# A selective-scan stack on one core: delta's matmul moved one slot later, one stream piece moved from slot 0 to slot 3, statistics of the finished sums one slot later

## The chip, the cores and the metric

The kernel runs on one core of a Trainium2 chip. The metric is device time in microseconds (us), the median of several executions. The core has five engines that matter here: PE (TensorE, matmuls), DVE (VectorE), ACT (ScalarE), POOL (GpSimd) and SP (SyncE, which here only issues DMAs).

## What is computed

The input x is (16, 192, 64, 64) in float32. Four layers follow each other, each `x = x + layer(group_norm(x))`:

- layer 0: a small per-channel network with tanh (a likelihood), evaluated at x - 0.5 and x + 0.5;
- layer 1: a 5-point shift and a 960 to 192 channel matmul;
- layer 2: four selective scans over the 4096 pixels, row-wise and column-wise, each in both directions (K = 4 directions, N = 16 states per channel);
- layer 3: depthwise convolutions, a channel mix, batch norm over all images, and a clip.

The scans are what the change touches. Cut to the core:

```python
delta = softplus(dts + dt_projs_bias)
def step(h, inp):
    d, u, Bt, Ct = inp
    dA = exp(d[..., None] * A)
    h = dA * h + (d * u)[..., None] * Bt[:, :, None, :]
    y = einsum('bkdn,bkn->bkd', h, Ct)
    return (h, y)
```

The outputs of the four directions are added, with the column-wise ones transposed back.

## The kernel before, in words

Two images form a pair: 2 x 192 channels are NT = 3 tiles of 128 partitions. For each of the 8 pairs `scans` runs layer 2 and, in the same loop, the *front* (statistics, layers 0 and 1, projection and split) of the next pair; then `layer3` runs. The first front runs alone before the loop, and the last pair has no front beside its scans. A last pass over all pairs does the batch norm and the clip.

**Slots and blocks.** `scans` walks over `todo`: tile j, direction k in the order 1, 3, 0, 2, and 4 chunks of LC = 1024 pixels. That is 48 *blocks* t of 16 *slots* n, one slot per state, so 768 slots s a pair. Within `scans` every engine keeps program order (`_InOrder`), so the loop from line 998 is an order written out by hand for each queue. One slot does, in this order:

- SP: `load_c(s + 2)`, the row of C broadcast to 128 partitions (tile cb, 4 buffers); in some slots also `load_bp`, `load_dt`, `load_xc`;
- DVE: `product(s)`, delta*u times B, in place in PSUM (tile pbt, 2 buffers), then whatever was handed to `E.later` (`E.between()` drains it), then the scan (`scan(s)`, tile h, 8 buffers);
- ACT: a copy of the scan's last column to `state`, then `decay(s + 3)`, the exponential dA (3 buffers);
- POOL: h times cb in place, and in every fourth slot a DMA that adds h of the slot before to it;
- PE: `spread(s + 2)`, two matmuls that spread B's row over the partitions into pbt;
- PE and ACT: `add_up(s - LATE)` with LATE = 4: the matmuls with the identity add h to `ysum` in PSUM; for the block's last state an ACT copy takes ysum to X or Xt. `ysum` has one buffer[...]. This call is made in slot 3 for the last state of the block before, and in slot 5 for the first sum of the block itself.

**Delta.** `step_rest(t + 1)` (lines 867 to 888) prepares the next block's delta: two matmuls into `v`, which takes the same PSUM buffer as `ysum` (tag "ysum"), an ACT softplus with bias to `delta` (with its own activation table, loaded before it, and the table of exp and tanh loaded again after it), and, at the next call in slot 8, `du` = delta*u on POOL. It is called in slot 3, right after `add_up` (lines 1023 to 1030). `load_dt(t + 2)` stands in slot 4 at the head of the loop; the tile `dt` has one buffer, which v reads.

**The stream.** `fr` is the next pair's front, a generator that yields pieces (lines 1032 to 1041). In layer 0 a piece is a quarter of a unit of 128 rows x 512 pixels: PE matmuls of two f32 products, the ACT tanhs or copies after them, and in places row loads by SP, a norm on ACT or a sigmoid. Slot 0 takes two layer-0 pieces, slots 3 and 5 none, all others one, and in slots 0 and 12 the statistics that a piece leaves behind are issued at once. In the other stages slots 0, 4, 8 and 12 take two units, 3 and 5 none, others one (a layer-1 matmul is half a unit, a projection step 0.36).

**Finishing.** When all four directions of a tile j are summed, `finish(j - 1)` (lines 963 to 980) adds Xt, transposed, to X in four parts: on POOL for the first two tiles, on DVE for the last. One step of it is made per slot from slot 5 on. Two steps after each add it hands the part's bn_stats (DVE) to `E.later`; after the last one it stores X by SP.

Of the kernel before, what the change touches and what calls it, by code (L numbers as in the profile page):

```python
# [104 lines left out]
def conv_preact_kernel(ctx: ExitStack, tc: tile.TileContext, a: dict):  # L105
# [5 lines left out]
    def row_tiles(ap):  # L111
        return ap.rearrange("(j p) l -> p j l", p=P)
# [199 lines left out]
    def image(ap):  # L312
        return ap.rearrange("p (h w) -> p h w", w=HW)

    def columns(ap):
        return ap.rearrange("p (h w) -> p w h", w=HW)
# [465 lines left out]
    def scans(i, o, st3, nxt):  # L782

        E = _Engines(tc, True)
        with ExitStack() as es:
# [14 lines left out]
            X = one.tile([P, L], F32, name="X")  # L800
# [12 lines left out]
            def seq(t, k, at, n):  # L813


                v = image(t) if k % 2 == 0 else columns(t)
                return v[:, at // HW : (at + n) // HW, :]

            def load_bp(t):
                if t < T:  # L820
                    j, k, at, first = todo[t]
                    bps[t] = two.tile([BP, LC], BF16, name="bp")
                    E.sp.dma_start(out=bps[t], in_=o.bp[k, :, at : at + LC])

            def load_dt(t):
                if t < T:
                    j, k, at, first = todo[t]
                    dts[t] = one.tile([32 + RD, 512], F32, name="dt")
                    src, r = (o.dtp, RD * (k // 2)) if k % 2 else (o.dt, RD * (2 + k // 2))
                    for h in range(2):  # L830
                        E.sp.dma_start(
                            out=dts[t][32 * h : 32 * h + RD, :],
                            in_=src[r : r + RD, at + 512 * h : at + 512 * h + 512],
                        )
# [6 lines left out]
            def norm_xn(j):  # L841
                if j < NT:
                    normalise(E.dve, xns[j], xns[j], o.gm, o.rstd, j)

            def load_xc(t):
                if t < T and todo[t][1] == 0:
                    j, k, at, first = todo[t]
                    xcs[t] = one.tile([P, LC], F32, name="xc")
                    E.sp.dma_start(out=xcs[t], in_=row_tiles(o.x2)[:, j, at : at + LC])

            def load_c(s):
                t, n = divmod(s, N)
                j, k, at, first = todo[t]
                cb = cbs[s] = cp.tile([P, LC], F32, name="cb")
                src, row = (o.c, 64 + 16 * k) if k % 2 == 0 else (o.cp, 16 * (k - 1))
                for b, rows in {
                    0: ((0, slice(0, P)),),
                    1: ((0, slice(0, 64)), (1, slice(64, P))),
                    2: ((1, slice(0, P)),),
                }[j]:  # L860
                    r = row + N * b + n
                    E.sp.dma_start(
                        out=cb[rows, :],
                        in_=src[r : r + 1, at : at + LC].to_broadcast([rows.stop - rows.start, LC]),
                    )

            def step_rest(t):


                j, k, at, first = todo[t]  # L870
                dt = dts.pop(t)
                v = py.tile([P, LC], F32, name="v", tag="ysum")
                for h in range(2):
                    rows = slice(32 * h, 32 * h + RD)
                    E.pe.matmul(
                        v[:, 512 * h : 512 * h + 512],
                        dtw[rows, k, j, :],
                        dt[rows, :],
                        start=True,
                        stop=True,  # L880
                    )
                delta = two.tile([P, LC], F32, name="delta")
                E.table(SOFTPLUS)
                E.act.activation(delta, v, AF.Softplus, bias=dtb[:, k, j : j + 1])
                yield
                du = two.tile([P, LC], F32, name="du")
                E.gps.tensor_tensor(image(du), image(delta), seq(xns[j], k, at, LC), ALU.mult)
                made[t] = delta, du

            def decay(s):  # L890
                t, n = divmod(s, N)
                j, k, at, first = todo[t]
                dA = dAs[s] = da.tile([P, LC], F32, name="dA")
                E.table(TANH)
                E.act.activation(dA, made[t][0], AF.Exp, scale=a_neg[:, k, j, n : n + 1])
# [14 lines left out]
            def product(s):  # L910
                E.dve.tensor_tensor(pbs[s], made[s // N][1], pbs[s], ALU.mult)

            def scan(s):
                t, n = divmod(s, N)
                j, k, at, first = todo[t]
                if (j, k) not in state:
                    state[j, k] = sp_.tile([P, N], F32, name="state")
                dA, pbt, cb = dAs.pop(s), pbs.pop(s), cbs.pop(s)
                back = k >= 2
                flip = slice(None, None, -1) if back else slice(None)  # L920
                h = hs[s] = hp.tile([P, LC], F32, name="h")
                v = state[j, k][:, n : n + 1]
                E.dve.tensor_tensor_scan(
                    h[:, flip], dA[:, flip], pbt[:, flip], 0.0 if first else v, ALU.mult, ALU.add
                )
                E.act.copy(v, h[:, 0:1] if back else h[:, LC - 1 : LC])
                E.gps.tensor_tensor(h, h, cb, ALU.mult)
                if n % 4 == 1:
                    E.gps.dma_start(out=h, in_=hs[s - 1], accum_op=ALU.add)
# [32 lines left out]

            def finish(j):

                for c in range(4):
                    x = X[:, 1024 * c : 1024 * c + 1024]
                    eng = E.gps if j < NT - 1 else E.dve
                    eng.tensor_tensor(
                        image(x), image(x), columns(Xt)[:, 16 * c : 16 * c + 16, :], ALU.add
                    )  # L970
                    yield
                    yield

                    def stats(c=c):
                        for h in range(2 * c, 2 * c + 2):
                            E.dve.bn_stats(st3[:, j, h, :], X[:, 512 * h : 512 * h + 512])

                    E.later(stats)
                yield
                E.sp.dma_start(out=row_tiles(x3_d[i])[:, j, :], in_=X)  # L980

            load_xn(0)
# [12 lines left out]
            kind = None  # L995
            fin = iter(())
            gstep = iter(())
            for s in range(total):
                t, n = divmod(s, N)
                j, k, at, first = todo[t]  # L1000
                if s + 2 < total:
                    load_c(s + 2)
                if n == 2:
                    load_bp(t + 1)
                if n == 4:
                    load_dt(t + 2)
                if n == 6:
                    load_xc(t + 1)
                product(s)
                E.between()  # L1010
                scan(s)
                if s + 3 < total:
                    decay(s + 3)
                if s + 2 < total:
                    spread(s + 2)
                if (t + 2) % (K * NC_) == 0 and n == 14:
                    load_xn(j + 1)
                if (t + 1) % (K * NC_) == 0 and n == 5:
                    norm_xn(j + 1)
                if n > 4:  # L1020
                    next(fin, None)

                if n == 3:
                    add_up(s - LATE)
                    if s >= LATE and (s - LATE + 1) % (K * NC_ * N) == 0:
                        fin = finish(j - 1)
                    gstep = step_rest(t + 1) if t + 1 < T else iter(())
                    next(gstep, None)
                elif n == 8:
                    next(gstep, None)  # L1030

                if kind == "l0":
                    for _ in range({0: 2, 3: 0, 5: 0}.get(n, 1)):
                        kind = next(fr, None) if kind == "l0" else kind
                        if n in (0, 12):
                            E.between()
                elif n not in (3, 5):
                    done = 0
                    while done < (1.99 if n % 4 == 0 else 0.99) and kind != "l0":
                        kind = next(fr, 1)  # L1040
                        done += kind if isinstance(kind, float) else 1
                if n != 3:
                    add_up(s - LATE)
# [293 lines left out]
```

## Time and profile before

| what | value |
| --- | --- |
| median of 3 executions | 28266.48 us (28245.82 to 28275.6) |
| profiled execution | 28295.17 us, span 28293.1 us |
| mean granted TensorE clock | 0.904 |
| DVE busy | 24223.9 us (86%) |
| PE busy | 23483.5 us (83%) |
| POOL busy | 20787.2 us (73%) |
| ACT busy | 16092.7 us (57%) |
| scans (DVE) | 6144 x, 2346 ns (with state) or 2285 ns (first chunk) |
| products (DVE) | 6144 x 1211 ns |
| adds of X and Xt on POOL | 64 x 3133 ns |
| softplus (ACT) | 384 x 1113 ns |
| activation table loads | 1104 x 1283 ns |

Pairs 0 to 6 take about 2998 us each from the first scan to the last, pair 7, without a front beside it, 2790 us. Seen from a pair's first scan, layer 0 of the next pair runs from some 107 to 1680 us, layer 1 from 1783 to 2290 us, the projection to 2475 us and the split to 2590 us.

How to read the lines: a line of the timeline gives start and duration in us, engine, line of the kernel (L64 is the helper that keeps program order, so one goes by the tiles' names), output<-inputs, shape, and in brackets the engine's idle time before it with what ended it. A line of the waits gives engine and tile, what it waited for, the total in us, the number of times, and the longest.

### The profile page before, as it was taken

To read this page: it belongs to the slowest core of one execution; us is meant where nothing else is said; L and a number is where in the kernel's file an instruction comes from. 1 tells how busy PE (TensorE), PEld (TensorE's weight loads), DVE (VectorE), ACT (ScalarE), POOL (GpSimd) and SP (SyncE) were. 2 spreads that over 40 slices of the span, in tenths; PEclk is the share of its full clock that TensorE was granted. 3 is DMA by queue.
4 is the path that set the end of the run, shared out by engine and by line. 5 is a ranking of instruction groups with operands and counts; after the bars stand their busy time and mean duration, and the time that the engine had idled before them with its cause. 6 is when DMAs were issued, how large, how long until landed. Compare 5 with 4: busy or idle time off the path is not lost. (4 is left out here: it accounts for less than half of the span.)

```text
span 28293.1 us, 208020 instructions
## 1 busy us (share of the span) xinstructions
PE 23483.5 (83%) x57140; PEld 9639.0 (34%) x57140; DVE 24223.9 (86%) x15397; ACT 16092.7 (57%) x23037; POOL 20787.2 (73%) x10440
## 2 busy tenths in 40 slices
PE   8799977999689986999779997799968998766663
PEld 4343323333233332333324332333323333222221
DVE  0399988998889988999989998899988998899994
ACT  7377445774467643775547744577446764344433
POOL 2388876887768876788768887688777887677772
PEclk9899988999899998999889998899989999888886
DMA  4479864897568973888748986489756897367765
GB/s 101 133 219 220 213 199 139 220 218 211 159 180 222 218 215 116 219 218 220 210 125 218 219 215 198 136 220 219 213 162 176 220 219 212 115 189 191 191 182 232
DMA packets 2008001, 5447.99 MB, mean 193 GB/s; under 512 B 550393, under 2 KB 550617, under 8 KB 1989425
## 3 DMA queue, kind: packets, MB, share of 16 engines
q1 hardware_dynamic: 1782192, 4578.95, 56.1%
q0 software_dynamic: 221184, 805.40, 14.9%
q10 hardware_dynamic: 3456, 50.33, 0.4%
q8 instruction: 455, 7.45, 0.1%
q14 instruction: 714, 5.84, 0.1%
HBM read 3896.19 MB, written 329.51 MB: 149 GB/s over the span
## 5 line engine op out<-in xcount | busy, mean ns | idle before, releaser
L64 POOL TENSOR_TENSOR h<-h,cb 128x1024 f32<-128x1024 f32 x6144 | 14853.6, 2465 | 4470.5 <-ACT state L64 3854.4
L64 DVE TENSOR_TENSOR_SCAN h<-dA,state,pbt 128x1024 f32<-128x1024 f32 x4608 | 10811.0, 2346 | 659.1 <-ACT dA L64 97.5
L64 PE MATMUL ysum<-h,ident 128*128 128x512 f32 x18432 | 9459.7, 638 | 191.6 <-DMA h<-h 144.7
L64 DVE TENSOR_TENSOR pbt<-du,pbt 128x1024 f32<-128x1024 f32 x6144 | 7441.2, 1211 | 852.4 <-PE pbt L64 812.1
L64 ACT ACTIVATE dA<-delta,t_alog 128x1024 f32<-128x1024 f32 x6144 | 7034.8, 1146 | 6.6
L64 PEld LDWEIGHTS ysum<-h,ident 128*128 128x128 f32 x18432 | 3780.8, 206 | 4474.2 <-issue 3926.6
L64 ACT COPY state<-h 128x1 f32<-128x1 f32 x6144 | 1141.0, 186 | 6533.9 <-DVE h L64 6508.4
L64 PE MATMUL pbt<-bp,pick 96*128 96x512 bf16 x8192 | 2729.3, 418 | 1942.8 <-DVE h L64 1931.8
L64 DVE TENSOR_TENSOR_SCAN h<-dA,pbt 128x1024 f32<-128x1024 f32 x1536 | 3509.0, 2285 | 181.5 <-DVE pbt L64 30.8
L64 PE MATMUL p<-t,wts 96*128 96x512 f32 x5376 | 2783.4, 618 | 164.0 <-ACT t L64 163.0
L64 PE MATMUL p<-m,wms 128*96 128x512 f32 (+1 forms) x5376 | 2720.3, 609 | 12.0 <-ACT lu L64 12.0
L64 ACT ACTIVATE t<-p,bias 96x512 f32<-96x512 f32 x2688 | 1803.6, 678 | 1162.8 <-PE p L64 1151.6
L64 PEld LDWEIGHTS <-pick 96*128 96x128 bf16 x8192 | 715.6, 102 | 4759.1 <-DVE h L64 2927.7
L1104 POOL TENSOR_TENSOR l_g<-l_g,l_m 128x1024 f32<-128x1024 f32 x672 | 1614.3, 2404 | 454.4 <-ACT l_g L1100 349.0
L64 PE MATMUL l_p<-l_xp,w1s 128*128 128x512 f32 x3920 | 1868.7, 609 | 0.0
L1127 DVE SCALAR_TENSOR_TENSOR l_p<-xp,wc,l_p 128x1024 f32<-128x1024 f32 x1248 | 1589.7, 1287 | 266.6 <-PE l_p L1121 235.8
L64 PE MATMUL pbt<-bp,pick_mix 96*128 96x512 bf16 x4096 | 1302.3, 401 | 569.8 <-DVE h L64 564.9
L64 POOL DMA_DIRECT2D h<-h x1536 | 1354.3, 882 | 495.1 <-POOL h L64 429.8
L1109 PE MATMUL l_p<-xp,diag 128*128 128x512 f32 x2688 | 1293.2, 641 | 331.9 <-DVE l_y L1127 281.2
L64 PEld LDWEIGHTS p<-t,wts 96*128 96x128 f32 x5376 | 1032.6, 195 | 1335.9 <-issue 903.1
L64 ACT ACT_TABLE_LOAD x1104 | 1416.4, 1283 | 19.3
L64 POOL TENSOR_TENSOR du<-delta,xn 128x1024 f32<-128x1024 f32 x384 | 1039.1, 2706 | 452.4 <-ACT delta L64 452.4
(219 smaller groups left out, 17710.1 us busy)
## 6 DMA issues: line engine op xcount, KB each, us to landing
cb<-cp_d SPq DMA_DIRECT2D x2048, 512.0 KB
cb<-c_d SPq DMA_DIRECT2D x2048, 512.0 KB
h<-h POOLq DMA_DIRECT2D x1536, 512.0 KB, 7.0
cb<-cp_d SPq DMA_DIRECT2D x2048, 256.0 KB
cb<-c_d SPq DMA_DIRECT2D x2048, 256.0 KB
m<-l_xn SPq DMA_DIRECT2D x3072, 128.0 KB
bp<-bp_d SPq DMA_DIRECT2D x384, 192.0 KB
f0x<-in_x SPq DMA_DIRECT2D x96, 512.0 KB
```

Of the source, the lines that this page charges most:

```text
L64: return self._tc.keep_in_program_order(call(*args, **kw))
L1104: nc.gpsimd.tensor_tensor(g, g, m, ALU.add)
L1109: nc.tensor.matmul(ps[:, cs], diag[:, j, t, :], window(j, 16 * c + 8 * h, 8, tap), start=(t == 0), stop=False,)
L1127: nc.vector.scalar_tensor_tensor(image(y if tap is TAPS[-1] else ps), window(j, 16 * c, 16, tap), factor(j, tap), image(ps), ALU.mult, ALU ...
```

## The change

Three things. The call of `step_rest(t + 1)` that issues the matmuls into `v` and the softplus goes from slot 3, right behind `add_up`, to slot 4, behind that slot's `spread(s + 2)`; the call that issues `du` stays in slot 8. Slot 3 now takes a stream piece (after `add_up`); slot 0 takes one layer-0 piece and not two, and outside layer 0 slot 4 takes one unit and not two. The immediate `E.between()` after pieces of slots 0 and 12 goes, so their statistics are issued after the next product. `finish` becomes ten steps: the adds stay in steps 0, 2, 4 and 6, the statistics go from steps 2, 4, 6 and 8 to steps 3, 5, 7 and 9, and the store of X comes a step later.

```diff
             def finish(j):
 
-                for c in range(4):
+                def add(c):
                     x = X[:, 1024 * c : 1024 * c + 1024]
                     eng = E.gps if j < NT - 1 else E.dve
                     eng.tensor_tensor(
                         image(x), image(x), columns(Xt)[:, 16 * c : 16 * c + 16, :], ALU.add
                     )
-                    yield
-                    yield
-
-                    def stats(c=c):
-                        for h in range(2 * c, 2 * c + 2):
-                            E.dve.bn_stats(st3[:, j, h, :], X[:, 512 * h : 512 * h + 512])
-
-                    E.later(stats)
-                yield
+
+                def stats(c):
+                    for h in range(2 * c, 2 * c + 2):
+                        E.dve.bn_stats(st3[:, j, h, :], X[:, 512 * h : 512 * h + 512])
+
+                for at in range(10):
+                    if at in (0, 2, 4, 6):
+                        add(at // 2)
+                    if at in (3, 5, 7, 9):
+                        E.later(lambda c=at // 2 - 1: stats(c))
+                    yield
                 E.sp.dma_start(out=row_tiles(x3_d[i])[:, j, :], in_=X)
...
                 if n == 3:
                     add_up(s - LATE)
                     if s >= LATE and (s - LATE + 1) % (K * NC_ * N) == 0:
                         fin = finish(j - 1)
+                elif n == 4:
                     gstep = step_rest(t + 1) if t + 1 < T else iter(())
                     next(gstep, None)
                 elif n == 8:
                     next(gstep, None)
 
                 if kind == "l0":
-                    for _ in range({0: 2, 3: 0, 5: 0}.get(n, 1)):
+                    for _ in range({5: 0}.get(n, 1)):
                         kind = next(fr, None) if kind == "l0" else kind
-                        if n in (0, 12):
-                            E.between()
-                elif n not in (3, 5):
+                elif n != 5:
                     done = 0
-                    while done < (1.99 if n % 4 == 0 else 0.99) and kind != "l0":
+                    while done < (1.99 if n in (0, 8, 12) else 0.99) and kind != "l0":
                         kind = next(fr, 1)
                         done += kind if isinstance(kind, float) else 1
```

## The prediction

> **What bounds the kernel now.** First the page's busy shares, then three stretches of pair 0 and of the last pair (which has no stream beside its scans), in the view of busy time by stage:
>
> ```profile
> PE 23483.5 (83%) x57140; PEld 9639.0 (34%) x57140; DVE 24223.9 (86%) x15397; ACT 16092.7 (57%) x23037; POOL 20787.2 (73%) x10440
> ```
>
> ```profile
> 1321.00:2891.00 1570.00, 1492.16 (x3780) 624.56 (x3779) 1441.21 (x850) 1242.69 (x1842) 1299.79 (x656) 0.97 0.86 220
> 24780.00:27550.00 2770.00, 1920.63 (x4185) 715.79 (x4184) 2651.01 (x1543) 1159.14 (x1710) 2104.59 (x1007) 0.83 0.69 190
> ```
>
> The columns are PE, PEld, DVE, ACT, POOL, the granted clock, DMA. In the last pair DVE is 96% busy: it bounds. In the layer-0 stretch (first line) PE is at 95% and DVE at 92%: two engines of nearly equal load, and a stall of one reaches the other. I then went through the trace slot by slot. A slot is one product and one scan; the groups give 1211 + 2346 ns, 3.56 us. Mean slot: 3.63 us in pair 7, 3.85 in the layer-0 stage (2863 slots in seven pairs, some 179 blocks of 16), so a block takes 61.6 us there. DVE's idle time before the products in that stage is 2.5 us a block: 0.31, 0.40 and 0.86 us before products 4, 5, 6, 0.14 before product 3, 0.40 before 8, nothing before most. The waits of DVE name the releaser, and the timeline shows one such place (block 23 of pair 1):
>
> ```profile
> DVE pbt L64 <- PE pbt L64: 812.1, 862, 9.7
> ...
> DVE st L64 <- POOL X L64: 115.6, 44, 4.1
> ```
>
> ```profile
> 6019.19 0.18 ACT L64 COPY state<-h 128x1 f32<-128x1 f32 x1
> ...
> 6020.32 0.99 ACT L64 COPY Xt<-ysum 128x1024 f32<-128x1024 f32 x1
> 6021.33 1.28 ACT L64 ACT_TABLE_LOAD   x1
> ...
> 6021.37 1.13 PE L64 MATMUL v<-dt,t_dtw 12*128 12x512 f32 x4 [2.87 <-ACT Xt L64]
> ...
> 6022.43 0.61 PE L64 MATMUL pbt<-bp,pick_mix 96*128 96x512 bf16 x2
> 6022.54 0.72 SPq L64 DMA_DIRECT2D dt<-dt_d  x2
> 6022.63 1.11 ACT L64 ACTIVATE delta<-v,t_dtb 128x1024 f32<-128x1024 f32 x1
> ...
> 6023.07 1.23 DVE L64 TENSOR_TENSOR pbt<-du,pbt 128x1024 f32<-128x1024 f32 x1 [1.61 <-PE pbt L64]
> ```
>
> v shares the one ysum buffer in PSUM, so PE stands 2.87 us until ACT has copied the finished sum; the next spread is queued behind v, and product 6 comes 1.61 us late. Over the layer-0 blocks v waits 1.41 us on average. The short windows around this place give a granted clock of 1.00 before and 0.58 in the 4 us after. In the trace's clock records 149 half-clock stretches (mean 4.15 us) begin in the layer-0 stage, 85 of them within 4 us after a v.
>
> [...] Here stretches follow waits of 1.1 to 2.9 us[...] The trace has 1.28 us and the softplus 0.02 us behind it; I use 1.28.
>
> **The change, part by part.** PE work in a layer-0 block, from starts of neighbouring records (0.43 us each; an f32 matmul has two, 0.86 us): spread 0.43, add_up 1.72 in three slots of four, the first of a block on average 3.44, stream piece 1.72, v 1.06.
>
> (a) *A piece from slot 0 to slot 3.* PE per slot before: 3.87 us in slots 13, 14, 15, 0, 1, 2; 3.21 in 3; 2.15 in 4. Against DVE's 3.6, six slots in a row put PE 6 x 0.27 = 1.6 us behind, then v's wait adds 1.41. The spreads show it: their delay after the scan that frees their buffer rises from 0.6 us (spread 15) to 3.2 (spread 5) and 4.2 (spread 6), and about 2.9 is what DVE bears. After: slot 0 has 2.15, so the backlog is gone there; spread 5 comes some 1.25 us after scan 3. The work is the same, 15 pieces a block (outside layer 0: 18 units a block before and after). ACT's two-piece lag after slot 0 (state copies 1.0 us behind their scan at n=0, 3.5 at n=1) goes too. The piece's row loads on SP move with it: past load_c of three slots and load_bp, each held by buffers anyway; charge 0.
>
> (b) *v after spread 6.* With scan 3 at 0 and slots of 3.6: add_up's matmuls end at 5.75, the copy at about 7.0, PE does the piece until 7.5 and spread 6 until 8.0, so v does not wait: 1.41 us of PE and most of the slow clock behind it (85 x 4.15 / 2 / 179 = 1.0 us of PE a block) are gone. softplus now stands behind state 4, the decay for 7 and a table load: 8.4 + 0.2 + 1.15 + 1.28, so it runs from 11.15 to 12.25. *The new wait*: add_up's first matmuls of the next sum (slot 5) need v read; PE would be there at 11.3 and waits about 1.0 us. Behind it on PE stand spread 8 and the slot-6 piece; DVE waits for spread 8 if it is over 2.9 us late. It is 1.25 + 0.27 + 1.0 = 2.5 late, in the passes with k=0 (two matmuls more than average) 4.2. Bounds of this wait: 0 (pair 7: ACT without pieces, delta done at 9.7 and PE there at 10.2) and 3.5 us (ACT lag as at n=3 now, 3.1, with a norm piece of 1.4 in front); I take 1.0. Two table loads a block remain. SP holds load_dt(t+2), and what is queued behind it, until v has read dt; it does so already (the SP line at 6022.54, after v's end), and v comes 1.3 us earlier in layer 0 and about 1 us later elsewhere; the cb tiles behind it are needed three slots later: 0.
> Sum for (a)+(b) in layer 0: 1.7 us before products 3 to 6 fall to about 0.2; 0.6 before 8 to 10 rise to about 0.9; fewer slow stretches 0.2: 1.4 us x 179 = **250 us**. The other stages: layer 1 loses 0.4 us a block before product 7 to v's 1.1 us, 56 blocks: 25. The projection loses 7.3 us once a pair before product 7, where slot 4's two units hold three ACT passes behind the softplus; with one unit in each of 3 and 4, half of it: 7 x 3.6 = 25. The split loses some 7.6 us before product 12, where PE waits for the h sum delayed by the same double slot 4: half, 7 x 4 = 28. In pair 7 v's wait reaches no product before 8: 0.
>
> (c) *Statistics one slot later.* 115.6 us of DVE idle before bn_stats of X, all of it in the 16 finishes on Pool; in pair 0 they are 2.87, 0, 4.05, 1.60 = 8.5 us. The adds (3.13 us on Pool) keep their slots. One slot is 3.6 us, but DVE that no longer waits arrives earlier: if Pool is never idle, 3.6 of 8.5 is won, if it follows DVE, all. 3.6 x 16 = 58 to 115; I take **70**. The x3 store moves from slot 14 to 15 on SP, far from its reader: 0.
>
> (d) *Statistics of a piece drained after the next product* instead of at once in slots 0 and 12: the same instructions on the same DVE queue, 0.
>
> Sum: 250 + 25 + 25 + 28 + 70 = 398. The profiled execution took 28295 us (span 28293), 29 over the median of 28266; on the median: **27868, I say 27870**.
>
> **Rivals.** *The wait only moves* (0.16): PE stands at the first sum as long as it stood at v, layer 0 wins nothing, the rest 148: 28120. For it: ACT at 79% in the stretch above; against: pair 7 and the shorter lag after slot 0. *Layer 0 comes down to DVE* (0.17): all 2.5 us go, 450 + 170 = 620: 27650. For it: the slow stretches start at v; against: PE's own 56.1 us of 57. *Nothing to speak of* (0.11): the new wait brings its own slow clock, and Pool's lag takes the 70 back: 28240. *Slower, by ACT in slots 3 to 5* (0.12): its work there rises from 10.05 to 11.45 us (one piece of 1.4) against 10.7 of DVE. The decay for 8 ends at 12.25 + 1.28 + 1.4 + 0.2 + 1.15 = 16.3, its scan is due at 18.0: 1.7 us. If ACT comes into slot 3 over 2.7 us late (1.0 is what I assume, 3.1 is measured now), DVE waits for dA, and pieces with a norm or a sigmoid (1.4 and 2.3 us more) make it 2 to 3 us; at 3 us a block against the 1.4 won, 179 x 1.6 = 286 lost less the 148 elsewhere: 28400. That the lag at slot 3 is a child of slot 0's double piece speaks against it.
>
> **How the numbers follow.** The forecast has 0.44. Faster, with the first two rivals: 0.77; within 0.2%, which is about what a measurement of this kernel can tell from no change: 0.11; slower: 0.12. The range leaves out the slow rival and the edges: low 27640 (all stalls of layer 0 and 170 elsewhere), high 28240. Without rivals the forecast's own range is 27740 to 28000, from the new wait at 0.3 to 2 us and (c) at 58 to 115.
>
> **What would show it.** Right: v with hardly any idle PE before it; products 4 to 6 in layer 0 under 0.1 us idle; a wait of PE at ysum for ACT's delta of some 1 us a block; fewer half-clock stretches; "DVE st <- POOL X" under 50 us; "DVE pbt <- PE pbt" near 450. Wrong: that last sum unchanged with the idle time before products 8 to 10 (the wait moved), or "DVE h <- ACT dA", now 116.8, at several hundred (ACT).

## The result: 0.9% faster, and the profile after

| | before | after |
| --- | --- | --- |
| median | 28267.1 us (4 runs) | 28006.5 us (28003.2 to 28009.4, 4 runs) |
| ratio | | 0.9909, 95% interval 0.9896 to 0.9922 |
| profiled execution | 28295.2 us | 28007.9 us, span 28006.0 us |
| mean granted TensorE clock | 0.904 | 0.912 |

The gain is 261 us where 397 were forecast. (The profiled execution of the kernel before took 28 us more than its median, that of the kernel after 1 us more, so gains read from the two traces come out somewhat higher.) The page's busy shares, and then the busy time by stage for the same two stretches as before (layer 0 beside pair 0, and the last pair, each moved to where it now lies):

```profile
PE 23305.0 (83%) x57140; PEld 9559.7 (34%) x57140; DVE 24196.3 (86%) x15397; ACT 16122.6 (58%) x23044; POOL 20813.2 (74%) x10440
```

```profile
1317.00:2864.00 1547.00, 1476.49 (x3780) 617.21 (x3779) 1437.12 (x850) 1245.86 (x1844) 1303.93 (x657) 0.99 0.87 223
24502.00:27260.00 2758.00, 1916.06 (x4180) 715.45 (x4180) 2642.63 (x1540) 1164.54 (x1708) 2100.44 (x1005) 0.83 0.69 190
```

The layer-0 stretch does the same 850 DVE instructions in 1547 us and not 1570; PE's busy time falls by 16 us for the same 3780 matmul records, at a mean clock of 0.99 and not 0.97. DVE works at 93%, up from 92. The waits of DVE, and below them one line of the kernel before:

```profile
DVE pbt L64 <- PE pbt L64: 619.6, 635, 7.7
...
DVE h L64 <- DMA h<-h: 132.6, 77, 5.8
...
DVE st L64 <- POOL X L64: 35.9, 20, 2.9
```

```profile
DVE h L64 <- DMA h<-h: 84.4, 61, 4.2
```

The first fell by 193 us (from 812.1) and the last by 80 (from 115.6), but the middle one, which the prediction did not look at, rose by 48. The place shown before, slots 3 to 5 of block 23 in pair 1, in the timeline after:

```profile
5959.38 0.59 PE L64 MATMUL pbt<-bp,pick_mix 96*128 96x512 bf16 x2
5959.40 0.99 ACT L64 COPY Xt<-ysum 128x1024 f32<-128x1024 f32 x1
...
5960.45 1.13 PE L64 MATMUL v<-dt,t_dtw 12*128 12x512 f32 x4 [0.47 <-ACT Xt L64]
5961.51 1.96 PE L64 MATMUL p<-m,wms 128*96 128x512 f32 x4
...
5962.97 1.28 ACT L64 ACT_TABLE_LOAD   x1
5963.28 2.37 SPq L64 DMA_DIRECT2D cb<-cp_d  x4
5963.30 0.60 PE L64 MATMUL pbt<-bp,pick_mix 96*128 96x512 bf16 x2
...
5964.26 1.11 ACT L64 ACTIVATE delta<-v,t_dtb 128x1024 f32<-128x1024 f32 x1
...
5965.43 1.12 PE L64 MATMUL ysum<-Xt,ident 128*128 128x512 f32 x2 [1.53 <-ACT delta L64]
```

The spread (the first line, pbt) goes ahead of v, v waits 0.47 us and not 2.87, no product waits here; the next sum's first matmul now waits 1.53 us for delta. Scans 3 to 9 of this block take 22.3 us from first to last start, against 24.0 before.

The trace slot by slot, for the 2863 layer-0 slots, as us a block of 16:

| idle time of DVE, us a block | before | after |
| --- | --- | --- |
| before products 3 to 6 | 1.70 | 0.17 |
| before products 8 to 10 | 0.58 | 1.15 |
| before the other products | 0.28 | 0.49 |
| before scans, over 0.1 each | 0.64 | 0.75 |
| before statistics | 0.35 | 0.13 |
| block | 61.54 | 60.60 |

PE waits 0.06 us a block at v (1.41 before) and 1.04 us at the first sum for delta (none before). Half-clock stretches, in which the granted clock is 0.5, fall in layer 0 from 149 (618 us) to 77 (338 us), and 2 of the 77, not 85 of 149, begin within 4 us after a v. In the whole program the new wait is:

```profile
PE ysum L64 <- ACT delta L64: 236.1, 193, 4.2
```

What is left before product 8 sits mostly in one direction: 3.19 us a block for k=0 (1.27 before), 0.40 for k=3, 0 for the other two. The new wait is as uneven: under 1 us in 129 of the 175 blocks, 1.0 to 1.9 us in 32, and 4.2 us in 14, which are blocks 9 and 25 of each pair. These 14 hold 90 of the 179 us for which DVE stands before product 8 in layer 0. The timeline of one of them, pair 0 block 25:

```profile
2754.77 1.28 ACT L64 ACT_TABLE_LOAD   x1
...
2756.06 1.06 ACT L64 ACTIVATE lu<-lu 128x1024 f32<-128x1024 f32 x1
...
2758.50 1.28 ACT L64 ACT_TABLE_LOAD   x1
2758.66 0.59 PE L64 MATMUL pbt<-bp,pick_mix 96*128 96x512 bf16 x2
...
2759.79 1.15 ACT L64 ACTIVATE dA<-delta,t_alog 128x1024 f32<-128x1024 f32 x1
...
2760.96 1.28 ACT L64 ACT_TABLE_LOAD   x1
2762.25 1.11 ACT L64 ACTIVATE delta<-v,t_dtb 128x1024 f32<-128x1024 f32 x1
...
2763.42 2.07 PE L64 MATMUL ysum<-xc,ident 128*128 128x512 f32 x2 [4.16 <-ACT delta L64]
...
2771.62 0.60 PE L64 MATMUL pbt<-bp,pick_mix 96*128 96x512 bf16 x2
...
2772.26 1.23 DVE L64 TENSOR_TENSOR pbt<-du,pbt 128x1024 f32<-128x1024 f32 x1 [7.57 <-PE pbt L64]
```

```profile
2755.00:2760.00 5.00, 4.26 (x13) 1.27 (x11) 4.80 (x3) 4.96 (x7) 1.68 (x2) 1.00 0.50 114
...
2765.00:2770.00 5.00, 5.00 (x8) 1.97 (x7) 0.00 (x0) 3.33 (x6) 3.48 (x3) 0.56 0.05 7
```

A sigmoid piece (lu) put two more table loads in front of delta: the one at 2754.77 for the sigmoid and the one at 2758.50, which brings exp back; the one at 2760.96, for the softplus, is there in every block. PE stands 4.16 us. The four matmuls that open the sum and the two that add the first h then take some 8 us, from 2763.42 to 2771.6. In the second view, 2765 to 2770, the clock is 0.56 (third column from the end) and DVE does nothing at all (0.00). Product 8 starts 7.57 us late.

### The profile page after: what moved, and what is told of

It reads as the page before. It is cut to its first block, busy times and chain, and to the rows that moved or that the text cites. A ratio compares the mean times of both kernels' runs of the same rounds, so it can differ in the third digit from the quotient of the medians.

```text
span 28006.0 us, 208082 instructions
## 1 busy us (share of the span) xinstructions
PE 23305.0 (83%) x57140; PEld 9559.7 (34%) x57140; DVE 24196.3 (86%) x15397; ACT 16122.6 (58%) x23044; POOL 20813.2 (74%) x10440
## 5 line engine op out<-in xcount | busy, mean ns | idle before, releaser
L64 DVE TENSOR_TENSOR pbt<-du,pbt 128x1024 f32<-128x1024 f32 x6144 | 7434.8, 1210 | 658.0 <-PE pbt L64 619.6
L64 PE MATMUL p<-t,wts 96*128 96x512 f32 x5376 | 2707.6, 602 | 136.1 <-ACT t L64 135.9
L64 PE MATMUL p<-m,wms 128*96 128x512 f32 (+1 forms) x5376 | 2653.6, 595 | 0.9 <-ACT lu L64 0.3
```

Source lines behind the costliest of these rows:

```text
L64: return self._tc.keep_in_program_order(call(*args, **kw))
```

## Experiments

Twelve kernels in three groups. The kernel before had medians of 28261, 28255 and 28259 us beside them.

**The parts alone.** *c_only* takes the new `finish` alone.

```diff
-                    yield
-                    yield
...
-                    E.later(stats)
+                for at in range(10):
+                    if at in (0, 2, 4, 6):
+                        add(at // 2)
+                    if at in (3, 5, 7, 9):
+                        E.later(lambda c=at // 2 - 1: stats(c))
+                    yield
```

Expected: 

> Only the statistics one slot later, everything else as before. Theory (POOL partly follows DVE): the 115.6 us that DVE waits for POOL X in the statistics of X fall to some 40, and 50 to 80 us are won: 28187 to 28217. Rival (POOL is never idle there and only moves its lag into the sums): the wait falls but PE waits longer for h, 28250 to 28267.

Measured 28243 us, ratio 0.9995 (0.9987 to 1.0003): no gain that can be told from none. *no_c* is the change with the old `finish`.

Expected: 

> The change without its finishing part. Theory (the parts add up): 50 to 80 us above the changed kernel's 28006, so 28056 to 28086, with the DVE wait for POOL X back at about 115. Rival (the finishing part does nothing beside the others, since POOL's lag gives it back): 28000 to 28020.

Measured 27981 us, 0.9899 (0.9884 to 0.9914): not above the changed kernel but 25 us below it (the intervals of the two ratios overlap, so these 25 us are not clear of noise). The theory missed twice. Where the gain goes is in the 18 slots from slot 4 of a block with a finish (mean of pairs 0 to 6; the second tile's fall in layer 1). The statistics wait less, 8.5 to 4.6 us a finish for the first tile and 7.3 to 3.2 for the second, c_only against before. For the first tile the stretch gets 4.8 us shorter; for the second the scans wait 9.6 us and not 5.0, and it gets 1.1 us longer: 26 us over seven pairs, where 55 us of waits for the statistics have gone. The waits of DVE in c_only show what rose:

```profile
DVE h L64 <- DMA h<-h: 120.3, 76, 9.5
```

It was 84.4: scans wait for an h tile that a late accumulating DMA still holds. In the finishing blocks of c_only POOL's product ends up to 16.6 us after its scan (12.0 before), so the DMA behind it starts that late. Why no_c is faster than the changed kernel, if it is, these stretches do not say: in the changed kernel they are 1.4 us shorter than in no_c for the first tile and 2.0 us longer for the second, 4 us over seven pairs.

*v_only* moves v and the softplus to slot 4 and leaves the pieces; *piece_only* moves the pieces and leaves v in slot 3, ahead of the piece. For v_only, against the kernel before:

```diff
+                elif n == 4:
                     gstep = step_rest(t + 1) if t + 1 < T else iter(())
```

and, for piece_only,

```diff
-                    for _ in range({0: 2, 3: 0, 5: 0}.get(n, 1)):
+                    for _ in range({5: 0}.get(n, 1)):
...
-                        if n in (0, 12):
-                            E.between()
-                elif n not in (3, 5):
+                elif n != 5:
...
-                    while done < (1.99 if n % 4 == 0 else 0.99) and kind != "l0":
+                    while done < (1.99 if n in (0, 8, 12) else 0.99) and kind != "l0":
```

Expected: 

> Delta's matmuls and softplus in slot 4 alone; pieces and statistics as before. Theory (two causes that work together): the wait of PE at v falls under 0.2 us a layer-0 block and product 6 no longer waits, but products 3 to 5 keep 0.85 us from slot 0's double piece, and ACT, 3 us late from the same double piece, makes the softplus later, so PE waits 2 us at the first sum and product 8 over 1 us: some 60 us won, 28170 to 28230. Rival 1 (v's wait is the whole cause): 200 us won, 28070. Rival 2 (the double piece is the whole cause): 28260 or slower.

Expected: 

> The piece moved from slot 0 to slot 3 (outside layer 0 a unit from slot 4 to slot 3) and its statistics drained after the next product, with v still in slot 3 ahead of the piece; statistics of X as before. Theory (two causes): products 3 to 5 lose their 0.85 us, product 6 keeps 0.9 us or more because v still waits 1 us and the piece is now behind it; some 100 us won, 28140 to 28190, half-clock stretches after v remain. Rival 1 (v's wait is the whole cause): within 20 us of before, 28250 to 28287. Rival 2 (the double piece is the whole cause): 28070.

Measured: v_only 28140 us, 0.9958 (0.9945 to 0.9970); piece_only 28204 us, 0.9980 (0.9972 to 0.9989). Both lie outside the ranges of the theory, 30 us below the one and 14 above the other. The waits of PE, in the kernel before, v_only and piece_only:

```profile
PE v L64 <- ACT Xt L64: 261.6, 192, 2.9
```

```profile
PE v L64 <- ACT Xt L64: 140.2, 139, 2.5
```

```profile
PE v L64 <- ACT Xt L64: 266.1, 192, 3.0
```

Alone they bring 121 and 57 us, together (no_c) 280, which is 102 more than the sum: each needs the other. In v_only v still waits 0.97 us a layer-0 block (expected: under 0.2): without a piece in slot 3 PE reaches v before ACT has made the copy; product 6 waits no more, products 3 to 5 keep 0.72 us, as expected, and the wait of the first sum for delta, expected at 2 us a block, is nearly absent (5.9 us in the whole program). In piece_only products 3 to 5 keep 0.11 us, product 6 waits 1.75 us (0.86 before), because v's wait of 1.35 us is still there and the piece stands behind it. So v's move takes the spread out from behind the wait, and the piece in slot 3 is what covers the copy. Rival 2 fails in both kernels, rival 1 in piece_only; v_only does not test rival 1, since most of v's wait is left in it. The size of the 102 us is less sure than its sign. The scans of v_only wait more for h buffers than those of the kernel before (84.4 us) or of piece_only (68.7):

```profile
DVE h L64 <- DMA h<-h: 149.8, 97, 5.6
```

The next group shows that this wait depends on a choice of the build that edits elsewhere move, and no run takes this choice out of v_only, piece_only or the kernel before.

**The remaining wait, and h tiles.** *spread_open* takes the matmuls that open a sum out of slot 5.

```diff
-                if n == 6:
+                if n == 10:
                     load_xc(t + 1)
...
                 if n != 3:
                     add_up(s - LATE)
+                if n in (8, 12):
+                    open_up(s, n // 4 - 2)
```

`open_up` issues the matmuls with xc, skip or the old X and Xt that `add_up` issued at n == 1; the sum now begins with the first h.

Expected: 

> The changed kernel, with the matmuls that open a block's sum (xc and skip for k=0, the old X or Xt otherwise) taken out of slot 5 and issued in slots 8 and 12, which have no matmul of a sum; the load of xc goes from slot 6 to slot 10. Theory (what is left in layer 0 is product 8, late because up to four opening matmuls stand on PE ahead of spread 8, on top of the wait for delta): its 0.98 us a block falls under 0.25, some 130 us won over the changed kernel, 27850 to 27900. Rival (the wait for delta alone makes product 8 late): 27980 to 28010.

Measured 28086 us, 0.9942 (0.9929 to 0.9954), 80 us slower than the changed kernel and outside theory and rival. Product 8 did what the theory says (0.98 to 0.31 us), but scan 13 waits 1.12 us a block that it did not wait before. The waits of DVE:

```profile
DVE h L64 <- DMA h<-h: 249.2, 112, 6.5
```

The addresses in the built programs tell why. The eight h buffers are not taken in turn: the build gives a scan the buffer of the scan 5 to 9 slots earlier, and in spread_open scan 13 gets that of scan 8 in 56 of 182 layer-0 blocks (in the changed kernel in none). h 8 is read by the DMA that adds it to h 9, which lands some 16 us after scan 9. The mean idle time before a scan by that distance, over the slots of pairs 0 to 6:

| slots since the buffer's last scan | 5 | 6 | 7 | 8 | 9 |
| --- | --- | --- | --- | --- | --- |
| before, us | 0.39 | 0.26 | 0.17 | 0.11 | 0.10 |
| c_only | 0.62 | 0.28 | 0.18 | 0.11 | 0.10 |
| after | 0.75 | 0.26 | 0.23 | 0.11 | 0.10 |
| spread_open | 1.34 | 0.23 | 0.21 | 0.11 | 0.12 |

*h9* gives the changed kernel nine buffers (`pool("l2h", 9)`).

Expected: 

> The changed kernel with nine h buffers and not eight. Theory (the statistics' gain was given back because POOL, late after its adds, holds h tiles, so that scans of the finishing blocks wait for a free one): the waits of DVE h for DMA h<-h, 132.6 us in the changed kernel, fall under 60, 30 to 70 us won, 27940 to 27975. Rival (the late h is waited for by PE's sums anyway): 27995 to 28015, the wait only changes its name.

Measured 27951 us, 0.9893 (0.9879 to 0.9906), 55 us below the changed kernel, as the theory has it, with this left of the wait that was 132.6 us:

```profile
DVE h L64 <- DMA h<-h: 24.4, 10, 4.8
```

*soft_first* puts v and the softplus ahead of slot 4's decay.

```diff
                 scan(s)
+                if n == 4:
+                    spread(s + 2)
+                    gstep = step_rest(t + 1) if t + 1 < T else iter(())
+                    next(gstep, None)
                 if s + 3 < total:
                     decay(s + 3)
-                if s + 2 < total:
+                if n != 4 and s + 2 < total:
                     spread(s + 2)
...
-                elif n == 4:
-                    gstep = step_rest(t + 1) if t + 1 < T else iter(())
-                    next(gstep, None)
```

Expected: 

> The changed kernel with spread 6, v and the softplus ahead of slot 4's decay. Theory (delta's lateness on ACT costs PE 1.05 us a layer-0 block at the first sum): delta comes 1.2 us earlier, the waits of ysum for ACT delta, 236 us in all, fall under 100, some 50 us won, 27940 to 27970. Rival 1 (dA for slot 7 now stands behind both table loads and DVE waits for it): DVE h <- ACT dA rises over 200 us, 28030 or more. Rival 2 (the opening matmuls, not delta, make product 8 late): 27995 to 28010.

Measured 27850 us, 0.9860 (0.9845 to 0.9875): 156 us below the changed kernel, three times what was expected. The waits of DVE:

```profile
DVE pbt L64 <- PE pbt L64: 408.5, 466, 5.2
```

PE's wait for delta falls from 1.04 to 0.22 us a layer-0 block, product 8's from 0.98 to 0.22 (k=0: 3.19 to 0.82), and the half-clock stretches from 77 to 35. Product 8 alone gives 138 of the 156 us (179 us of idle time before it in layer 0 become 40). What the wait itself and what the slower clock behind it takes of this, the run does not separate. The price that rival 1 named is small: DVE waits 163.5 us in all for dA, 111.5 before this edit. *open_no_c* is spread_open with the old `finish`.

Expected: 

> The openings of the sums in slots 8 and 12 as in spread_open, and the finishing part as in the kernel before. Theory (the two are independent, and the new finishing part costs 25 us in the changed kernel): 25 us below spread_open, 27825 to 27875. Rival (with PE less late the later statistics pay): 20 to 60 us above spread_open.

Measured 28048 us, 0.9928 (0.9916 to 0.9941): 38 us below spread_open, the third time that the new `finish` is no help, and the clearest (the fastest execution of spread_open took 28079 us, the slowest of open_no_c 28060). (The absolute figures expected fail with spread_open's.)

**h buffers in turn.** One tag for each buffer makes the distance always eight.

```diff
-            hp = pool("l2h", 8)
+            hp = pool("l2h", 1)
...
-                h = hs[s] = hp.tile([P, LC], F32, name="h")
+                h = hs[s] = hp.tile([P, LC], F32, name="h", tag=f"h{s % 8}")
```

*after_rot* is the changed kernel with it, *no_c_rot* the change with the old `finish`, *open_rot* spread_open, *soft_rot* soft_first.

Expected: 

> The changed kernel with h tiles that take their eight buffers in turn (one tag each), so that a scan always takes the buffer of the scan eight slots before; the build's own choice gives distances of 5 to 9 slots. Theory (scans wait where the distance is 5 to 7: 0.75, 0.26, 0.23 us on average, some 258 us over the 0.1 of distance 9): these waits fall to 0.12, DVE h for DMA h<-h falls from 132.6 to under 40, 150 to 230 us won, 27780 to 27860. Rival (the late tile is then waited for by PE or ACT all the same): 27960 to 28010.

Expected: 

> The change without its finishing part, h buffers in turn. Theory (the later statistics lost their gain only to scans that take a buffer five slots old): with the buffers in turn they pay, and this kernel is 40 to 70 us above after_rot. Rival (POOL's lag gives the gain back in other places too): within 20 us of after_rot, or below it.

Expected: 

> spread_open with h buffers in turn. Theory (spread_open lost because its build gave scan 13 the buffer of scan 8 in 56 layer-0 blocks, which a DMA still reads): the wait of scan 13, 1.12 us a block, falls to 0.1, the wait of product 8 stays at 0.3, and the kernel is 60 to 120 us below after_rot. Rival (the openings in slots 8 and 12 themselves delay the sums): at or above after_rot.

Expected: 

> soft_first with h buffers in turn. Theory (the two gains are of different waits and add): 130 to 220 us below soft_first, 27630 to 27720. Rival: DVE is near its own 3.56 us and the engines behind it are late elsewhere, 27780 or more.

| kernel | median, us | ratio to before (95%) | same without the turn |
| --- | --- | --- | --- |
| after_rot | 27963 | 0.9894 (0.9881 to 0.9908) | 28006 |
| no_c_rot | 27956 | 0.9891 (0.9878 to 0.9905) | 27981 |
| open_rot | 27908 | 0.9875 (0.9862 to 0.9889) | 28086 |
| soft_rot | 27810 | 0.9842 (0.9828 to 0.9855) | 27850 |

open_rot confirms the reading of spread_open: scan 13 waits 0.10 us, the kernel gains 178 us, and ends 55 us below after_rot (60 to 120 expected). after_rot gains 43 us where 150 to 230 were expected: DVE stands 134 us less before scans than in the changed kernel, but 76 us more before products. The waits of DVE in after_rot:

```profile
DVE pbt L64 <- PE pbt L64: 686.1, 595, 8.2
```

It was 619.6. And no_c_rot is level with after_rot: even with the buffers in turn the later statistics bring nothing that can be told. In the finishing blocks of after_rot the second tile's scans wait 1.4 us where those of the changed kernel wait 8.5, but PE waits 1.9 us a finish for the DMA of h (0.1 in the changed kernel). The range of the rival is met; its reason, that POOL is late and its lateness is waited for by whoever comes next, is read from these waits. soft_rot, the fastest here, is 448 us below the kernel before. It gains 40 us over soft_first where 130 to 220 were expected. Against after_rot it is 153 us faster, so the gain of putting the softplus first (156 us in soft_first) does not come from the choice of buffers.

## Why the prediction was right in direction and high in size

By its own steps, in us over the seven pairs (measured: the stage's slots times the change of its mean slot):

| step | predicted | measured |
| --- | --- | --- |
| (a)+(b) layer 0 | 250 | 2863 x (3.847 - 3.788) = 169 |
| layer 1 | 25 | some 878 x (4.039 - 3.990) = 43 |
| projection | 25 | some 192 x (4.633 - 4.356) = 53 |
| split | 28 | some 147 x (4.236 - 4.241) = -1 |
| (c) statistics | 70 | c_only: 18, not told from 0; no_c: -25, not clear of noise |
| sum | 398 | 261 |

The (c) row lies inside the stage rows, so the column is not added up; the stages' 264, with 18 in the slots of no stage named here and in the first statistics, make the 281 us by which the eight pairs' scans get shorter in the two traces (the medians have 261). In the trace of no_c, which has (a) and (b) without (c), the same slots of layer 0 get 188 us shorter, so of the 250 a quarter is missing. The sum came nearer than its rows, and that is luck in part: layer 1 and the projection brought 96 us where 50 were forecast, the split and (c) nothing where 98 were.

*Right.* The two causes in layer 0, the wait at v and slot 0's double piece: products 3 to 6 went from 1.70 to 0.17 us (0.2 predicted). v's wait is gone (0.06 us), the new wait at the first sum is 1.04 us (1.0 taken), and there are fewer half-clock stretches. That the mean of the new wait came out is luck in part, as the spread from under 1 to 4.2 us shows. (In the prediction's working of it the sum 8.4 + 0.2 + 1.15 + 1.28 gives 11.03 and not 11.15, which changes nothing.) No loss from draining the pieces' statistics later shows in the traces. POOL's waits for the rows of C (cb), which SP loads behind `load_dt`, rose from 348 to 403 us; no run says whether that costs time. Projection: product 7's 7.2 us became 0.26, but product 3 now waits 1.70 in the slot that got a unit; more was won than the half that was forecast.

*Mis-sized, layer 0: the cost of the new wait.* The prediction had 0.9 us before products 8 to 10 where 1.15 came, and it let 0.3 elsewhere stand, where 0.49 came. It worked with the mean wait of 1.0 us. soft_first shows what it was worth: with most of it gone 156 us were won. The wait is not long on average but comes as 4.2 us in two blocks of each pair, in front of six matmuls; within 4 us after the first of them a half-clock stretch begins in 6 of these 14 blocks of layer 0, and in 3 of the 32 with 1.0 to 1.9 us. The blocks with k=0, whose spread 8 the prediction had 4.2 us late, were then averaged into the 0.9: they alone cost 3.19 - 1.27 = 1.9 us in each of their 49 blocks, 94 us. And the 0.2 us a block for fewer slow stretches was counted on top of DVE's idle time; the rows of the idle-time table fall by 0.86 us where the block falls by 0.94, so hardly more than 0.08 us came on top.

*Wrong, (c).* The step "if Pool is never idle, 3.6 of 8.5 is won, if it follows DVE, all" took the DVE wait for the cost. It bounded the gain at 58 us from below and did not let it be nothing, though a rival of the prediction had POOL's lag take the 70 back. The wait did fall, to 35.9 us; c_only brought 18 us that cannot be told from none, and beside the other parts the old `finish` is as good (no_c, no_c_rot) or 38 us better (open_no_c). By the waits, DVE met POOL's lag at the statistics (115.6 us before); without that it meets it at the next h tile (84.4 to 120.3 us in c_only), or PE meets it at the sum (1.9 us a finish in after_rot).

*Wrong, the split.* Product 12 went from 3.9 to 0.06 us as reasoned. But product 8 went from 1.7 to 5.3 us in one block of each pair and from 0 to 3.4 in the block before it. In front of both PE waits for delta, 2.8 and 3.8 us in the mean of the pairs; in pair 0 the second is

```profile
3663.75 3.63 PE L64 MATMUL ysum<-Xt,ident 128*128 128x512 f32 x4 [3.76 <-ACT delta L64]
...
3669.57 1.23 DVE L64 TENSOR_TENSOR pbt<-du,pbt 128x1024 f32<-128x1024 f32 x1 [2.90 <-PE pbt L64]
```

That is (b)'s new wait, which the prediction had charged to layer 0 alone. Product 4 went from 0 to 1.5 us, behind a wait of PE for the DMA of h, and product 0 keeps 3.2 of its 3.9 us behind the same wait. No experiment took the split apart.

The rival "the wait only moves" was half true, in the blocks with k=0; the slower one did not come: in layer 0 state 3 is copied 1.1 us after its scan, as assumed, and DVE's wait for dA did not rise (116.8 to 111.5 us).

Still open: in layer 0 a half-clock stretch begins within 4 us after 85 of the 175 waits of v in the kernel before, and after 9 of the 46 waits for delta of 1 us and more in the changed kernel, but no kernel held the wait and changed the clock alone, so the cause is not shown. Where (c)'s gain goes when the h buffers are in turn is read from the waits of one profiled execution each, not from an edit that removes POOL's lag; a slower rhythm of the adds on POOL was not tried.

## What to carry to other kernels

A wait for an engine that lags can be worth next to nothing as long as the lag itself stays (in c_only 55 us of waits over seven pairs went, and 18 us of time that cannot be told from none): before pricing a moved consumer, ask who reads the late engine's next result. A short mean wait in front of a long burst on the near-bound engine should be priced by its worst blocks, not by its mean (1.04 us here, with 90 of the 179 us before product 8 in 14 of 175 blocks). Two edits that cover each other are tested together: alone they brought 121 and 57 us of 280. When a small reordering costs time where no dependency explains it, look up which buffer the build gave the waiting tile (scan 13 of spread_open, 1.12 us a block, was such a case).

## What the runs showed that was not expected

- Half-clock stretches (4.15 us in the mean) follow waits of PE of 1.1 to 2.9 us in a stage where PE is 95% busy. In layer 0 of the kernel before, one begins within 4 us after 23 of the 31 waits of v that are over 2 us, and after 62 of the 144 of 1 to 2 us; in v_only after 3 of the 143 under 1 us.
- The build's choice of h buffers moves with edits elsewhere, and is worth 178 us in one kernel (spread_open to open_rot) and 25 to 44 us in the others, of which the 25 (no_c) are hardly clear of noise.
- Putting the softplus ahead of one decay, 1.15 us of ACT work, gained 156 us, 0.6% of the kernel, and 153 us with the buffers in turn.
